# Numbering sorted tokens by partition first and chunk second, with running sums on GpSimd, in a convolution, attention and mixture-of-experts kernel

## The chip, the cores and the metric

The kernel runs on one core of one Trainium2 chip. The metric is device time in microseconds of one execution. The engines are named as the profile names them: PE (TensorE; its weight loads are PEld), DVE (VectorE), ACT (ScalarE), POOL (GpSimd) and SP (SyncE, which only issues transfers here).

## The reference, cut to what matters

The input is 32 images of 128 channels and 56 x 56 pixels, so 3136 tokens an image.

```
x = x + conv3x3(sign(groupnorm(x)), sign(w)) * Alpha
t = tokens of x                                    # 3136 an image, 128 wide
t = t + q(ln(t)) * sum over tokens of k(ln(t)) * v(ln(t))
...
p = softmax(ln(t) @ router_w + router_b)           # 8 experts
top_p, top_i = top_k(p, 2); top_p /= sum(top_p)
t = t + sum over the two of top_p * (ln(t) @ expert_w[top_i] + expert_b[top_i])
```

Each token goes through the two experts of its own choice, so it belongs to one of 8 * 7 / 2 = 28 unordered pairs of experts. In what order tokens of one pair are worked on is free.

## The kernel before, in words

**Tiling.** The tokens of an image stand in 25 chunks of up to 128 tokens, one token a partition (`n_ck` = 25). The layers up to the router run image by image: convolution in 7 strips (L642), transposes to tokens, statistics, the gram matrix (L744), the projection (L863), the router on DVE (L949 on).

**Two ways through the experts.** The first 8 or 12 chunks of an image, and all chunks of images 28 to 31, are done densely: all eight experts for each token, with gates that are 0 for six of them (`gated`, L1141, and `ff`, L1159). The other 17 chunks (images 0 to 15) or 13 chunks (images 16 to 27) are sorted by pair over a group of images (groups of 8, 8, 8 and 4): each token's row of 132 floats is written by an indirect transfer, which GpSimd issues, to its place in a buffer of rows in HBM (`scatter`, L1365, one for each chunk, 428 in all). Once a group is complete, tiles of 128 rows of one pair are read back, go through two experts alone (L1687), are stored, and are then fetched back into token order by another 428 indirect transfers (`gather`, L1444), turned (`back_turn`, L1459) and stored.

**The place of a token.** The steps that the change touches compute it, once for each of the 28 images with sorted chunks; `n_sort` is 17 or 13:

- `pair_of` (L1236, DVE): the number of the token's pair, and last `hot` (L1256): for each chunk 28 columns, 1 in the column of the token's pair, in bf16.
- `hot_blocks` (L1263): sums of four chunks of `hot`, on POOL in images 0 to 7 (three adds, L1268 and L1270), on DVE from image 8 on (one reduction, L1272).
- `places` (L1274, PE): for each chunk and pair the place of the next token in one PSUM tile of 504 or 392 columns. A product with the triangle `before` (L1278) counts the tokens on lower partitions of the same chunk; two products add the counts of the images before, as a high and a low bf16 part (L1281); products with `ones_h` (L1293) add earlier chunks, by single chunks within a block of four and by `hot_sum` for whole blocks: 17 of them for 17 chunks, 13 for 13. So places are numbered chunk by chunk, and within a chunk by partition.
- `count_on` (ACT, L1303 and L1304) and `count_rest` (DVE, L1307): the last 28 columns are the counts to carry on.
- `row_numbers` (DVE, L1309): `hot` times `places`, read from PSUM, summed over the 28 columns (L1315), gives the row (L1318).
- `row_add` (ACT) and `scatter` (POOL) follow.

`list_1` (L1550, DVE) reads the counts when the last image of a group is counted and lists the tiles.

**What sets the order.** Every engine runs its queue in order. The order of all queues comes from a planner, `in_order` (L116), which lays out 12116 steps by due times, costs and waits: each `at(due, key, engine, cost, do, after=, take=, free=)` declares a step, `take` and `free` the buffers of a ring such as the five PSUM banks `ps`. The costs are estimates written in the code: `hot_blocks` has 2.0 us on POOL and 0.048 * n_sort on DVE, `places` 0.3 + 0.08 * n_sort, a gather or a scatter 1.5 us. A step whose cost differs on the chip keeps its place in the queue; its engine or those after it then wait. Gathers land in a ring of `back` buffers (room for 12 in the plan), and at most four indirect transfers are under way at a time.

Of the kernel before, what the change touches and what calls it, by code (L numbers as in the profile page):

```python
# [54 lines left out]
C = 128  # L55
# [20 lines left out]
    mybir.EngineType.Pool,  # L76
    mybir.EngineType.SP,
}
ON_POOL = 8
NEWTON = 3  # L80
IN_FLIGHT = 4
HELD, LOADS, LOAD_LANDS = 3, 4, 10.0
# [103 lines left out]
def conv_attn_moe_kernel(  # L186
# [357 lines left out]
    def plan_image(i: int):  # L544
# [688 lines left out]
        hot = hot_all[:, most - n_sort :, :]  # L1233
        n_full = n_sort // PER

        def pair_of():  # L1236
            high, low, pair = (
# [16 lines left out]
            yield  # L1254
            shape = [C, n_sort, N_PAIR]
            nc.vector.tensor_tensor(  # L1256
                hot[:, :n_sort, :],
                mark.unsqueeze(2).to_broadcast(shape),
                pair_no.unsqueeze(1).to_broadcast(shape),
                ALU.is_equal,  # L1260
            )

        def hot_blocks():  # L1263
            t = hot[:, : n_full * PER, :].rearrange("p (b k) q -> p b k q", k=PER)
            total = hot_sum[:, :n_full, :]
            with nc.allow_low_precision(reason="numbers up to four"):
                if i < ON_POOL:
                    nc.gpsimd.tensor_tensor(total, t[:, :, 0], t[:, :, 1], ALU.add)  # L1268
                    for k in range(2, PER):
                        nc.gpsimd.tensor_tensor(total, total, t[:, :, k], ALU.add)  # L1270
                else:
                    nc.vector.tensor_reduce(total, t.rearrange("p b k q -> p b q k"), AX.X, ALU.add)  # L1272

        def places():  # L1274


            p = ps.tile([C, n_sort + 1, N_PAIR], F32, tag="ps", name=f"places_{i}")
            nc.tensor.matmul(p, lhsT=before, rhs=hot, start=True, stop=False)  # L1278
            if not first_of_group:
                for j in range(2):  # L1280
                    nc.tensor.matmul(  # L1281
                        p,
                        lhsT=ones_h[:1],
                        rhs=count_h[:1, j].unsqueeze(1).to_broadcast([1, n_sort + 1, N_PAIR]),
                        start=False,
                        stop=False,
                    )

            counted = [(hot[:, c, :], c + 1, min(n_sort + 1, c // PER * PER + PER)) for c in range(n_sort)]
            counted += [(hot_sum[:, b, :], (b + 1) * PER, n_sort + 1) for b in range(n_full)]  # L1290
            counted = [(t, lo, hi) for t, lo, hi in counted if lo < hi]
            for t, lo, hi in counted:
                nc.tensor.matmul(  # L1293
                    p[:, lo:hi, :],
                    lhsT=ones_h,
                    rhs=t.unsqueeze(1).to_broadcast([C, hi - lo, N_PAIR]),
                    start=False,
                    stop=lo == counted[-1][1] and hi == counted[-1][2],
                )
            d["places"] = p  # L1300

        def count_on():
            nc.scalar.copy(count, d["places"][:, n_sort, :])  # L1303
            nc.scalar.copy(count_h[:, 0], d["places"][:, n_sort, :])  # L1304

        def count_rest():
            nc.vector.tensor_sub(count_h[:, 1], count, count_h[:, 0])  # L1307

        def row_numbers():  # L1309
            shape = [C, n_sort, N_PAIR]  # L1310
            own = spool.tile(shape, F32, tag="own", bufs=1, name=f"own_{i}")
# [50 lines left out]
        def scatter(c):  # L1362
# [15 lines left out]
            after=[("route_3", i), ("row_numbers", i - 1), ("places", i - 1), ("result_rows", i - 13)],  # L1378
        )
        at(  # L1380
            s + 132.5, ("hot_blocks", i), "POOL" if i < ON_POOL else "DVE",
            2.0 if i < ON_POOL else 0.048 * n_sort, hot_blocks, after=[("pair_of", i)],
        )
        at(
            s + 133, ("places", i), "PE", 0.3 + 0.08 * n_sort, places,
            after=[("hot_blocks", i), ("count_rest", i - 1), ("list_1", group - 1)], take=["ps"],
        )
        at(s + 135, ("count_rest", i), "DVE", 0.10, count_rest, after=[("count_on", i)])
        at(s + 134, ("count_on", i), "ACT", 0.22, count_on, after=[("places", i)])
# [488 lines left out]
```

## Time and profile before

| | |
|---|---|
| median of 3 runs | 2259.04 us (2249.86 to 2283.94) |
| profiled execution | 2270.18 us |
| its span | 2268.4 us |
| granted TensorE clock, mean | 0.975 |
| POOL scatters (L1365) | 428, 524.3 us, mean 1225 ns |
| POOL gathers (L1444) | 428, 485.4 us, mean 1134 ns |
| DVE gating products (L1141) | 384, 450.7 us, mean 1180 ns |
| `hot` (L1256), `own` (L1313), `place` (L1315), medians | 590, 642, 650 ns |
| `count`, `count_h` (L1303, L1304), medians | 182, 188 ns |

The span is the time from the first to the last instruction in the trace. Busy time is the sum over an engine's own work; waits, branches and the issue of transfers on SP don't count[...]. "Idle before, released by" names what an engine waited for. Matmuls are pipelined, so several overlap within their stated lengths.

### The profile page before, as it was taken

The page shows a single profiled execution, that of the slowest core. Times are in us where ns is not written, and L with a number is a line of the kernel's source. Part 1 is how long each engine was busy: PE and PEld are TensorE (multiplying, and loading weights), DVE is VectorE, ACT ScalarE, POOL GpSimd, SP SyncE. Part 2 cuts the span into 40 slices and gives each one's busy share as a digit, 9 for nine tenths or more (in the row PEclk, how much of TensorE's full clock was granted, in tenths as well). Part 3 has the DMA queues.
Part 4 walks back from the last instruction along what each step waited for, and adds up shares of the span by engine and source line. Part 5 has one row for each costly group of instructions (what it writes and reads, how often), then busy time and mean ns, then how long its engine had stood idle before and what let it go on. Part 6 is the DMA issues. An engine that isn't in the chain of part 4 may idle for free.

```text
span 2268.4 us, 45320 instructions
## 1 busy us (share of the span) xinstructions
PE 2103.4 (93%) x12074; PEld 1449.1 (64%) x12074; DVE 1970.1 (87%) x6074; ACT 1531.2 (68%) x4917; POOL 1041.1 (46%) x1013
## 2 busy tenths in 40 slices
PE   5899999899999999789999999988999999999888
PEld 2666656557777776457676776655676666676544
DVE  4899999999989999688888889988898798789865
ACT  5667776668888887468777867655877776574311
POOL 3044443333433325466443644676654446233563
PEclk9989999999999999899999999999999999999999
DMA  4155544465665565377667766667767777878788
GB/s 166 30 175 177 167 153 141 138 184 184 203 186 165 176 181 168 110 219 252 194 202 220 226 198 202 215 214 240 225 195 232 217 203 247 249 214 270 222 278 273
DMA packets 324364, 448.58 MB, mean 198 GB/s; under 512 B 61832, under 2 KB 222128, under 8 KB 324112
## 3 DMA queue, kind: packets, MB, share of 16 engines
q1 hardware_dynamic: 294384, 382.80, 54.7%
q0 software_dynamic: 28144, 56.14, 8.2%
q10 hardware_dynamic: 1584, 6.75, 0.8%
q8 instruction: 102, 1.67, 0.3%
q14 instruction: 150, 1.23, 0.2%
HBM read 319.51 MB, written 126.00 MB: 196 GB/s over the span
## 4 chain that ended last, share of the span: by engine, by line
PE 42%; DVE 5%; DMA 3%; issue 2%; ACT 2%; another core or an unknown queue 1%; SPq 0%; POOL 0%; DVEq 0%; ACTq 0%; POOLq 0%
PE ff L1159 14%; PE to L1687 7%; PE cv L642 6%; PE q L863 3%; PE gram L744 3%; PE turn L1669 2%; PE back_ps L1459 2%; PE xt L667 2%; DVE gated L1141 1%; DMA back<-res,res_no 1%; PE l L1114 1%; DMA out_dram<-o 1%; PE ff L1153 1%; DMA bc<-gp 0%
## 5 line engine op out<-in xcount | busy, mean ns | idle before, releaser
L1365 POOL DMA_INDIRECT rows<-tok,row_no x428 | 524.3, 1225 | 570.5 <-ACT tok L1358 235.8
L1159 PE MATMUL ff<-gated,ew_d 128*128 128x512 f32 (+1 forms) x1536 | 711.5, 592 | 23.8 <-DVE gated L1141 19.8
L1444 POOL DMA_INDIRECT back<-res,res_no x428 | 485.4, 1134 | 464.1 <-PE back_ps L1459 264.1
L1141 DVE TENSOR_TENSOR gated<-tt,bc 128x1024 f32<-128x1024 f32 x384 | 450.7, 1180 | 92.2 <-PE ff L1159 29.9
L642 PE MATMUL cv<-xs,w_bin 128*128 128x440 bf16 (+3 forms) x2016 | 429.8, 362 | 18.5 <-ACT xs L599 10.0
L1159 PEld LDWEIGHTS ff<-gated,ew_d 128*128 128x128 f32 x1536 | 274.5, 193 | 258.6 <-issue 202.2
L1705 ACT ACTIVATE v<-to,t_in 128x128 f32<-128x128 f32 x528 | 255.3, 484 | 138.1 <-PE to L1687 74.6
L642 PEld LDWEIGHTS <-w_bin 128*128 128x128 bf16 x2016 | 200.1, 100 | 187.8 <-issue 38.3
L1687 PEld LDWEIGHTS to<-ew_s,turned 128*128 128x128 f32 x2112 | 260.8, 194 | 57.8 <-issue 32.4
L877 ACT ACTIVATE qs<-q,r 128x136 f32<-128x136 f32 (+1 forms) x800 | 247.6, 406 | 70.3 <-PE q L863 35.1
L1687 PE MATMUL to<-ew_s,turned 128*128 x2112 | 273.3, 279 | 18.2 <-ACT turned L1675 8.1
L735 ACT ACTIVATE y<-tok,r 128x128 f32<-128x128 f32 (+1 forms) x800 | 257.0, 428 | 24.3 <-PE gram L744 10.4
L863 PE MATMUL q<-move,x 128*128 128x144 f32 (+1 forms) x1600 | 239.9, 295 | 12.7 <-issue 3.7
L863 PEld LDWEIGHTS q<-move,x 128*128 128x128 f32 (+1 forms) x1600 | 213.6, 193 | 42.4 <-issue 21.1
L744 PEld LDWEIGHTS gram<-y 128*128 128x128 f32 (+1 forms) x1600 | 203.3, 192 | 53.9 <-issue 40.4
L744 PE MATMUL gram<-y 128*128 128x129 f32 (+1 forms) x1600 | 217.8, 281 | 12.9 <-issue 8.1
L682 DVE BATCH_NORM_STATS2 st<-tok 128x6 f32<-128x128 f32 (+1 forms) x800 | 185.4, 279 | 31.9 <-ACT tok L673 26.9
L1712 ACT ACTIVATE w<-to,t_in 128x128 f32<-128x128 f32 x528 | 208.6, 395 | 0.0
L893 DVE BATCH_NORM_STATS2 st<-tok 128x6 f32<-128x128 f32 (+1 forms) x800 | 198.1, 284 | 6.3
L673 ACT COPY tok<-xt 128x512 f32<-128x512 f32 (+1 forms) x224 | 121.2, 561 | 99.9 <-PE xt L667 71.6
L653 DVE SCALAR_TENSOR_TENSOR x<-cv,alpha_col,x 128x448 f32<-128x448 f32 x224 | 151.3, 676 | 40.1 <-PE cv L642 7.2
L890 DVE TENSOR_TENSOR tok<-tok,qs 128x408 f32<-128x408 f32 (+1 forms) x288 | 156.1, 542 | 29.4 <-ACT tok L882 24.1
(229 smaller groups left out, 2896.0 us busy)
## 6 DMA issues: line engine op xcount, KB each, us to landing
bc<-gp SPq DMA_DIRECT2D x368, 512.0 KB
x<-in_x_dram SPq DMA_DIRECT2D x116, 392.0 KB
t_in<-rows SPq DMA_DIRECT2D x528, 66.0 KB
res<-v SPq DMA_DIRECT2D x132, 256.0 KB
out_dram<-o SPq DMA_DIRECT2D x100, 256.0 KB
out_dram<-tt SPq DMA_DIRECT2D x92, 256.0 KB
rows<-zeros SPq DMA_DIRECT2D x116, 66.0 KB
rows<-tok,row_no POOLq DMA_INDIRECT x428
```

The costliest lines, as they stand in the source:

```text
L642: nc.tensor.matmul(cv[:, r0:r1, c0:c1], lhsT=w_bin[:, t, :], rhs=xs[:, b * ROWS + dy + r0 : b * ROWS + dy + r1, dx + c0 : dx + c1], start= ...
L735: nc.scalar.mul(y[:n, j, :C], d["tok"][:n, c, :C], d["r1"][:n, c : c + 1])
L744: nc.tensor.matmul(d["gram"], lhsT=y[:n, j, :C], rhs=y[:n, j, :], start=(c == 0), stop=(c == n_ck - 1),)
L863: nc.tensor.matmul(p[:n, k, :], lhsT=d["x"][:, c * C : c * C + n], rhs=move, start=True, stop=True,)
L877: nc.scalar.mul(qs[:n, k, :], p[:n, k, : C + N_EXP], d["r1"][:n, c : c + 1])
L1141: nc.vector.tensor_tensor(g[:, :, :n], d["tt", b][:, :n].unsqueeze(1).to_broadcast([C, 2, n]), d.pop(("bc", b, k))[:, :, :n], ALU.mult,)
L1159: nc.tensor.matmul(d["ff", b][:, :n], lhsT=ew_d[:, e * C : (e + 1) * C], rhs=g[:, j, :n], start=False, stop=(e == N_EXP - 1),)
L1365: dma = nc.gpsimd.indirect_dma_start(out=groups[group]["rows"], out_offset=bass.IndirectOffsetOnAxis(ap=d["row_no"][:n, c - n_dense : c - ...
L1444: dma = nc.gpsimd.indirect_dma_start(out=d["back", c][:n, :], out_offset=None, in_=groups[group]["res"][: quads_of(group) * WIDE, :], in_o ...
L1687: nc.tensor.matmul(p[:, k, j, :], lhsT=t[:, n * C : (n + 1) * C], rhs=ew_s[:, bass.ds(d["cols", q][j][n], C)], start=True, stop=True,)
L1705: nc.scalar.activation(d["v", q][:, n, :], p[:, k, 0, :], AF.Identity, bias=row[:, C + 2 : C + 3], scale=row[:, C : C + 1],)
L1712: nc.scalar.mul(d["w", q][:, n, :], p[:, k, 1, :], row[:, C + 1 : C + 2])
```

## The change

Places are numbered by partition first and by chunk second. POOL adds up `hot` chunk by chunk in `run`, 28 columns at a time (`run_on`, 17 or 13 adds, each of which reads what the one before it wrote), so that `run[:, c]` holds, for each partition, the tokens of each pair in earlier chunks, and the last one the total of the partition. `places` then needs only that last total: one product with `before` for the tokens on lower partitions, one with `ones_h` for the counts, and, but for the first image of a group, one product of 33 rows that adds the earlier images' counts, the high part from row 0 and the low part from row 32 of `count_h`. The PSUM tile has 56 columns. ACT copies both halves to `counts`, which frees the bank. POOL then adds the partition's start to all of `run` (`ranks`, one addition of 476 or 364 fp32 columns), and `row_numbers` multiplies `hot` with this from SBUF. `hot_blocks` and `hot_sum` are gone, on POOL as on DVE. The planner has costs of 0.20 (`RUN`) and 0.10 us (`RANK`) a chunk for the two new POOL steps, 0.25 for `places`, 0.35 for `count_on`.

In the changed program PE has 80 products for the places instead of 504. The planner lays out all queues again, so the order of other steps moves too. On POOL the adds and `ranks` stand ahead of an image's scatters; from image 14 on they stand between gathers of the group before. In the program each add but the first waits on a semaphore of POOL itself.

```diff
-ON_POOL = 8
+RUN, RANK = 0.20, 0.10
...
-    count = const.tile([C, N_PAIR], F32, name="count")
-    count_h = const.tile([C, 2, N_PAIR], BF16, name="count_h")
+    counts = const.tile([C, 2, N_PAIR], F32, name="counts")
+    count = counts[:, 1]
+    n_part = C // 4 + 1
+    count_h = const.tile([n_part, N_PAIR], BF16, name="count_h")
+    both = const.tile([n_part, C], BF16, name="both")
...
-    hot_all = const.tile([C, most + 1, N_PAIR], BF16, name="hot")
-    hot_sum = const.tile([C, most // PER, N_PAIR], BF16, name="hot_sum")
+    hot_all = const.tile([C, most, N_PAIR], BF16, name="hot")
+    run_all = const.tile([C, most + 1, N_PAIR], BF16, name="run")
 
     def prepare_sorted():
-        nc.gpsimd.memset(hot_all, 0.0)
-        nc.vector.memset(count_h, 0.0)
+        nc.gpsimd.memset(run_all[:, 0], 0.0)
+        nc.vector.memset(both, 0.0)
+        nc.vector.memset(both[:1], 1.0)
+        nc.vector.memset(both[n_part - 1 :], 1.0)
...
-        def hot_blocks():
-            t = hot[:, : n_full * PER, :].rearrange("p (b k) q -> p b k q", k=PER)
-            total = hot_sum[:, :n_full, :]
-            with nc.allow_low_precision(reason="numbers up to four"):
-                if i < ON_POOL:
-                    nc.gpsimd.tensor_tensor(total, t[:, :, 0], t[:, :, 1], ALU.add)
-                    for k in range(2, PER):
-                        nc.gpsimd.tensor_tensor(total, total, t[:, :, k], ALU.add)
-                else:
-                    nc.vector.tensor_reduce(total, t.rearrange("p b k q -> p b q k"), AX.X, ALU.add)
+        def run_on():
+
+            with nc.allow_low_precision(reason="numbers up to the chunks of an image"):
+                for c in range(n_sort):
+                    nc.gpsimd.tensor_tensor(run[:, c + 1], run[:, c], hot[:, c], ALU.add)
 
         def places():
-            p = ps.tile([C, n_sort + 1, N_PAIR], F32, tag="ps", name=f"places_{i}")
-            nc.tensor.matmul(p, lhsT=before, rhs=hot, start=True, stop=False)
+            p = ps.tile([C, 2, N_PAIR], F32, tag="ps", name=f"places_{i}")
             if not first_of_group:
-                for j in range(2):
...
+                nc.tensor.matmul(
+                    p,
+                    lhsT=both,
+                    rhs=count_h.unsqueeze(1).to_broadcast([n_part, 2, N_PAIR]),
+                    start=True,
+                    stop=False,
+                )
+            for j, lhs in enumerate((before, ones_h)):
+                nc.tensor.matmul(
+                    p[:, j], lhsT=lhs, rhs=run[:, n_sort], start=first_of_group, stop=first_of_group or j == 1
                 )
             d["places"] = p
 
         def count_on():
-            nc.scalar.copy(count, d["places"][:, n_sort, :])
-            nc.scalar.copy(count_h[:, 0], d["places"][:, n_sort, :])
+            nc.scalar.copy(counts, d["places"])
+            nc.scalar.copy(count_h, d.pop("places")[:n_part, 1])
 
         def count_rest():
-            nc.vector.tensor_sub(count_h[:, 1], count, count_h[:, 0])
+            last = slice(n_part - 1, n_part)
+            nc.vector.tensor_sub(count_h[last], count[last], count_h[last])
+
+        def ranks():
+            shape = [C, n_sort, N_PAIR]
+            d["own"] = spool.tile(shape, F32, tag="own", bufs=1, name=f"own_{i}")
+            nc.gpsimd.tensor_tensor(
+                d["own"], run[:, :n_sort], counts[:, 0].unsqueeze(1).to_broadcast(shape), ALU.add
+            )
 
         def row_numbers():
...
-            nc.vector.tensor_tensor(own, hot[:, :n_sort, :], d.pop("places")[:, :n_sort, :], ALU.mult)
+            nc.vector.tensor_tensor(own, hot, own, ALU.mult)
...
+            s + 132.5, ("run_on", i), "POOL", RUN * n_sort, run_on,
+            after=[("pair_of", i), ("places", i - 1), ("ranks", i - 1)],
...
+            s + 133, ("places", i), "PE", 0.25, places,
+            after=[("run_on", i), ("count_rest", i - 1), ("list_1", group - 1)], take=["ps"],
...
+            s + 134, ("count_on", i), "ACT", 0.35, count_on,
+            after=[("places", i), ("ranks", i - 1), ("list_1", group - 1)],
+            free=[("ps", ("places", i))],
...
+        at(s + 135, ("count_rest", i), "DVE", 0.08, count_rest, after=[("count_on", i)])
+        at(
+            s + 135, ("ranks", i), "POOL", RANK * n_sort, ranks,
+            after=[("count_on", i), ("row_numbers", i - 1)],
+        )
...
             s + 137, ("row_numbers", i), "DVE", [0.033 * n_sort, 0.034 * n_sort, 0.09], row_numbers,
-            after=[("places", i), ("count_on", i), ("scatter", i - 2, n_ck - 1)],
-            free=[("ps", ("places", i))],
+            after=[("ranks", i), ("scatter", i - 2, n_ck - 1)],
```

More of the change, by code (lines that the diff above doesn't have):

```diff
@@ L1232, in plan_image @@
         sort = slice(n_dense, n_ck)
-        hot = hot_all[:, most - n_sort :, :]
-        n_full = n_sort // PER
+        hot, run = hot_all[:, :n_sort], run_all[:, : n_sort + 1]
         def pair_of():
@@ L1256, in pair_of @@
             nc.vector.tensor_tensor(
-                hot[:, :n_sort, :],
+                hot,
                 mark.unsqueeze(2).to_broadcast(shape),
@@ L1274, in places @@
         def places():
-            p = ps.tile([C, n_sort + 1, N_PAIR], F32, tag="ps", name=f"places_{i}")
-            nc.tensor.matmul(p, lhsT=before, rhs=hot, start=True, stop=False)
+            p = ps.tile([C, 2, N_PAIR], F32, tag="ps", name=f"places_{i}")
             if not first_of_group:
-                for j in range(2):
[L1281 to L1298, printed above, removed]
+                nc.tensor.matmul(
+                    p,
[4 more added lines that the diff above has]
+                )
@@ L1302, in count_on @@
         def count_on():
-            nc.scalar.copy(count, d["places"][:, n_sort, :])
-            nc.scalar.copy(count_h[:, 0], d["places"][:, n_sort, :])
+            nc.scalar.copy(counts, d["places"])
+            nc.scalar.copy(count_h, d.pop("places")[:n_part, 1])
         def count_rest():
-            nc.vector.tensor_sub(count_h[:, 1], count, count_h[:, 0])
+            last = slice(n_part - 1, n_part)
[6 more added lines that the diff above has]
+            )
         def row_numbers():
-            shape = [C, n_sort, N_PAIR]
-            own = spool.tile(shape, F32, tag="own", bufs=1, name=f"own_{i}")
+            own = d.pop("own")
             place = spool.tile([C, n_sort], F32, tag="place", bufs=13, name=f"place_{i}")
-            nc.vector.tensor_tensor(own, hot[:, :n_sort, :], d.pop("places")[:, :n_sort, :], ALU.mult)
+            nc.vector.tensor_tensor(own, hot, own, ALU.mult)
             yield
@@ L1380, in plan_image @@
         at(
-            s + 132.5, ("hot_blocks", i), "POOL" if i < ON_POOL else "DVE",
-            2.0 if i < ON_POOL else 0.048 * n_sort, hot_blocks, after=[("pair_of", i)],
-        )
-        at(
-            s + 133, ("places", i), "PE", 0.3 + 0.08 * n_sort, places,
-            after=[("hot_blocks", i), ("count_rest", i - 1), ("list_1", group - 1)], take=["ps"],
-        )
-        at(s + 135, ("count_rest", i), "DVE", 0.10, count_rest, after=[("count_on", i)])
-        at(s + 134, ("count_on", i), "ACT", 0.22, count_on, after=[("places", i)])
+            s + 132.5, ("run_on", i), "POOL", RUN * n_sort, run_on,
+            after=[("pair_of", i), ("places", i - 1), ("ranks", i - 1)],
+        )
+        at(
+            s + 133, ("places", i), "PE", 0.25, places,
+            after=[("run_on", i), ("count_rest", i - 1), ("list_1", group - 1)], take=["ps"],
+        )
+        at(
[4 more added lines that the diff above has]
+        at(s + 135, ("count_rest", i), "DVE", 0.08, count_rest, after=[("count_on", i)])
+        at(
+            s + 135, ("ranks", i), "POOL", RANK * n_sort, ranks,
+            after=[("count_on", i), ("row_numbers", i - 1)],
+        )
         at(
             s + 137, ("row_numbers", i), "DVE", [0.033 * n_sort, 0.034 * n_sort, 0.09], row_numbers,
-            after=[("places", i), ("count_on", i), ("scatter", i - 2, n_ck - 1)],
-            free=[("ps", ("places", i))],
+            after=[("ranks", i), ("scatter", i - 2, n_ck - 1)],
         )
```

## The prediction

> **What bounds the kernel now.** I read the page's busy shares and 40 slices first, then busy time in five stretches, then the rows of the tiles that the change touches, and last the order of time around one image.
>
> ```profile
> PE 2103.4 (93%) x12074; PEld 1449.1 (64%) x12074; DVE 1970.1 (87%) x6074; ACT 1531.2 (68%) x4917; POOL 1041.1 (46%) x1013
> ...
> PE   5899999899999999789999999988999999999888
> ...
> POOL 3044443333433325466443644676654446233563
> ```
>
> PE is busy from the third slice to the end and its granted clock stands at 0.8 or more in every slice, so PE sets the pace: 165 us of the 2268.4 us span are idle, most of that at the start and in the last stretch. DVE is close behind (298 us idle), POOL has half its time free. The chain that ended last, followed back over the later half of the span, agrees: PE has 42% of the span in it, DVE 5%, POOL 0%; the lines it names are expert, conv, projection and gram products. What the change takes off PE is therefore worth nearly its own length, unless PE then waits for something new.
>
> The products for the places on PE alone, their busy time summed over five stretches that cover the span:
>
> ```profile
> sum 2269.00, PE 43.77; mean PE 8.75
> ```
>
> and by line (count: shortest/median/longest in ns, first and last start in us, forms):
>
> ```profile
> L1278 PE MATMUL places<-hot,before x28: 328/375/627, 110.5 to 1831.4; 128*128 128x504 bf16 x16, 128*128 128x392 bf16 x12
> L1281 PE MATMUL places<-count_h,ones_h x48: 325/372/382, 156.6 to 1831.9; 1*128 1x504 bf16 x28, 1*128 1x392 bf16 x20
> L1293 PE MATMUL places<-hot,ones_h x328: 174/189/279, 110.9 to 1832.4; 128*128 128x28 bf16 x64, 128*128 128x84 bf16 x56, 128*128 128x56 bf16 x44
> L1293 PE MATMUL places<-hot_sum,ones_h x100: 187/237/488, 111.6 to 1832.6; 128*128 128x280 bf16 x28, 128*128 128x168 bf16 x28, 128*128 128x56 bf16 x28, 128*128 128x392 bf16 x16
> ```
>
> So 504 products hold PE for 43.8 us, 1.9% of the span. PE's idle time before the first of them is 0.4 us in all 28 images together: their operands are there when PE comes to them.
>
> **What the added adds cost.** Today GpSimd sums one-hots for eight images only, three adds of 112 columns each:
>
> ```profile
> L1272 DVE TENSOR_REDUCE hot_sum<-hot x20: 707/730/928, 515.1 to 1829.2; 128x84 bf16<-128x336 bf16 x12, 128x112 bf16<-128x448 bf16 x8
> L1270 POOL TENSOR_TENSOR hot_sum<-hot_sum,hot x16: 384/432/1420, 107.5 to 452.7; 128x112 bf16<-128x112 bf16 x16
> L1268 POOL TENSOR_TENSOR hot_sum<-hot x8: 373/376/602, 107.0 to 451.7; 128x112 bf16<-128x112 bf16 x8
> ```
>
> And what happens around them, in order of time (start and length in us), for the first image and then for the second:
>
> ```profile
> 107.04 0.38 POOL L1268 TENSOR_TENSOR hot_sum<-hot 128x112 bf16<-128x112 bf16 x1 [78.57 <-DVE gate L981]
> 107.49 0.98 POOL L1270 TENSOR_TENSOR hot_sum<-hot_sum,hot 128x112 bf16<-128x112 bf16 x2
> ...
> 153.67 1.21 DVE L1141 TENSOR_TENSOR gated<-tt,bc 128x1024 f32<-128x1024 f32 x1
> 153.70 1.42 POOL L1270 TENSOR_TENSOR hot_sum<-hot_sum,hot 128x112 bf16<-128x112 bf16 x1
> 154.80 0.37 DVE L1346 TENSOR_TENSOR tok<-a,m_one 128x34 f32<-128x34 f32 x1
> ```
>
> Two things to see. Each add waits for the one before it: starts are 0.45 us apart where the add itself takes 0.38, a gap of 0.07. And GpSimd and DVE stop each other: an add that met the gating product (two SBUF inputs) took 1.42 instead of 0.38, and the next DVE instruction, half beneath the add, took 0.37 instead of its usual 0.18. Nearly every one of the 24 adds lengthens one DVE instruction by about 0.19 us.
>
> **What the Trainium skill says.** "GPSIMD Engine Reference", section 3.1, gives 4497 ns for a GpSimd add of 2048 fp32 elements, 2.2 ns an element; with it a 112-column add has 0.24 us of elements and 0.13 of fixed cost, which fits 0.376. Its section 8 (Key points) says that GpSimd shares its SBUF interfaces with VectorE and contends with instructions that have two SBUF inputs: the pair at 153.67 shows it. "Perfetto Trace Analysis", section "GPSIMD Engine Instruction", advises timing GpSimd by start-to-start spacing rather than by reported spans; so I price the adds by spacing.
>
> **The change part by part.**
>
> PE. Removed: 504 products, 43.8 us. Added: 80 (three an image, two in the four first of a group) of 28 or 56 columns. One such alone takes 0.19 us, and in a row they follow at 0.55/13 = 0.04 us (13 products in 0.55 us at 157.11); I take 0.19 + 2 x 0.10 = 0.39 an image, 11 us. Net **-33 us**, on the path. Bounds -28 (no overlap of the three) to -38 (full overlap).
>
> DVE. Removed: 20 reductions of 0.730, -14.6 us. The product of marks and places keeps its columns (0.64, now from SBUF), the subtraction its 0.18. Two small memsets at the start: nothing. Added: being stopped. 428 running adds that hold the port between 0.05 us (by columns, 28 of 112) and 0.19 us (all of it fixed), and 28 rank additions of 476 or 364 columns, 0.13 + 476 x 2.2 ns = 1.2 us (0.9); the planner's 0.10 a chunk, 1.7 us, is the upper bound. If DVE wants the port 7 times in 10: 428 x 0.10 x 0.7 + 28 x 1.1 x 0.7 = 30 + 22 = 52, from 15 to 90. Net about **+37 us on DVE**; it has 298 us idle, and its gating products feed PE, so I let a quarter through: +9, between 0 and +30.
>
> ACT. Two copies an image as before, 56 columns instead of 28 in one (0.18 now): nothing, hidden by 32% idle. The ps bank comes free at these copies, no longer at DVE's first part of row_numbers, 1 to 3 us sooner; the view of this tile lists 3.6 us in which PE waited for its readers, so this is worth -2, at most -4.
>
> POOL. The eight hot_sum sets go (11 us). 428 adds of 28 columns: by columns 0.376 - 84 x 2.2 ns = 0.19, plus the gap 0.07 = 0.27 us apart; no dearer than the 112-column ones, 0.45. DVE's traffic lengthened the 24 adds by 0.09 on average over 0.376; I take 0.32. That is 5.4 us for 17 chunks and 4.2 for 13, where the planner laid the queues out with RUN = 0.20: 3.4 and 2.6. Sum 137 us, ranks 31: POOL to some 1200 us, 53%. Queued behind run_on, which waits for DVE's marks, are scatters of the same image, and from image 14 on gathers of the group before; these have a ring of 12 back buffers ahead of PE, and POOL's longest wait is for PE (264 us, for the turning of those rows), so POOL runs ahead and the gathers keep their cover.
>
> The new wait. PE's products now need all of run_on, which starts when DVE's marks (L1256) end. Today the first product starts 1.7 to 7.7 us after the marks, 3.4 on average. The changed order puts it later by what run_on is planned to take beyond hot_blocks: 1.4 us in images 0 to 7 (3.4 for 2.0), 2.6 in 8 to 15 (3.4 for 0.8), 2.0 in 16 to 27 (2.6 for 0.6). PE is then there after 4.8, 6.0 and 5.4 us. At 0.32 us an add and 0.3 for two semaphore hops, run_on needs 5.7 us for 17 chunks and 4.5 for 13. So PE waits 0.9 us in each of the first 8 images (7), nothing on average in the next 8, but with a scatter of 1 to 2 us around it half a us (4), and in the last 12 some 0.3 by the same scatter and 0.3 for a gather that POOL is just issuing (7). About 18 us of waiting in the whole, queued behind which are conv, expert and gram products; ACT's copies and DVE's row_numbers wait the same time. Three quarters reach the end: **+13**, bounds 0 (0.27 us an add) to +86 (0.45, below).
>
> DMA. Rows go to other places in the same buffers, same count and size of packets (528 bytes a row): 0, with 10 us either way, since no run here shows other row orders. SP's steps are the same.
>
> Sum: -33 + 9 + 13 - 2 = **-13 us**. The profiled execution took 2270.18 us with its 2268.4 us span, 11 us above the median of the three runs shown, 2259.04 (2249.86 to 2283.94). -13 gives 2257 for it, and 2246 against the median.
>
> **The rivals.**
>
> 1. PE gets all of it. The adds run at 0.27, PE never waits, DVE's contention falls into its idle time and the 14.6 us of reductions and the banks shorten other engines' waits too: -38 - 10 - 4 = -52, 2207 us. For it: PE at 93%, 54% of POOL idle. Against it: the visible mutual stops.
>
> 2. The other side: GpSimd becomes the link that PE waits for. If an add takes 0.50 us (the spacing seen, 0.45, being fixed price rather than columns, and a little of DVE's interference), run_on needs 8.8 us and 6.8. PE waits 4.0 us in 8 images, 2.8 in 8 and 1.4 plus half a gather (0.65) in 12: 32 + 22 + 25 = 79. With DVE at +12, less 33: +58, 2317 us. It decides from an add of about 0.37 us on (break-even: waits of 35 us, three quarters of them through), and passes 2% at about 0.46. For it: 0.45 is the one spacing seen. Against it: that is for four times the columns.
>
> 3. The change does little because the planner's new order gives elsewhere what it takes: all queues are laid out anew from the first image. That gives between -20 and +20 beside the sum, and lies inside the first case.
>
> **How the numbers follow.** 2% is about what a measurement of this kernel can tell from no change: 45 us. The likeliest case (2246, own range 2215 to 2275, with the third rival in it) has 0.46, rival 1 0.34, rival 2 0.20. Faster by over 2% means below 2214: 0.34; slower, above 2304: 0.20. The range of 8 in 10 takes in most of rival 1 and what lies between the first case and rival 2, whose far part is left out: 2196 to 2304.
>
> **What would show it.** Right: products for the places near 10 us of PE in all; running adds starting 0.27 to 0.36 us apart; PE idle before the first product 10 to 30 us in total, put down to POOL; DVE's small instructions longer by some 0.1 us beside the adds, its busy time up by 20 to 50 us. Wrong: adds 0.4 us apart or more and PE idle there over 60 us (rival 2); no PE wait there and a PE busy time down by 33 with the span down as much or more (rival 1); or a difference that comes from stretches after image 27, where none of the changed steps run.

## Result, and the profile after

| | before | after |
|---|---|---|
| median, us | 2258.35 (4 runs, 2249.86 to 2283.94) | 2289.22 (4 runs, 2288.41 to 2296.36) |
| profiled execution / its span, us | 2270.18 / 2268.4 | 2296.36 / 2294.7 |
| granted TensorE clock, mean | 0.975 | 0.966 |
| PE busy without the places, us | 2059.6 | 2069.7 |
| PE busy with the places, us | 43.8 | 10.0 |
| PE idle (span less busy), us | 165.0 | 215.0 |

The ratio of after to before is 1.0156 (95% interval 1.0126 to 1.0186): the change makes the kernel slower by about 35 us. The forecast was 13 us faster. Ratios are of the means of those executions that are within 1.5% of the fastest of their kernel, so the 2283.94 of before is not in them (the medians of the table differ by 31 us), and the profiles of experiments 2 and 9 show an execution slower than that. The last three rows of the table add up to the span in each column, so they say where the 26 us between the two profiled executions come from: 34 less of places, 10 more of all other products, 50 more of idle time.

The page of the changed kernel, busy time by engine, then PE's 40 slices, then the shares of the chain that ended last:

```profile
PE 2079.7 (91%) x11650; PEld 1441.2 (63%) x11650; DVE 1982.4 (86%) x6056; ACT 1532.8 (67%) x4917; POOL 1194.4 (52%) x1445
...
PE   5889889988999999798999999899889988999888
...
PE 47%; DVE 30%; issue 6%; DMA 5%; ACT 5%; POOL 5%; another core or an unknown queue 2%; SPq 0%; DVEq 0%; ACTq 0%; POOLq 0%
```

PE's row, which was 9 almost throughout, has 8 in more slices of the stretch with sorting. The chain before was followed over the later half of its span alone, so its shares can't be compared with these; here POOL has 5%, nearly all of it the running adds.

The view of the tile `places`: rows of its products, then the time its engine sat idle before it, by releaser (us, times):

```profile
L1286 PE MATMUL places<-run,before x28: 174/174/188, 116.9 to 1852.0; 128*128 128x28 bf16 x28
...
L1278 PE MATMUL places<-count_h,both x24: 188/196/197, 162.0 to 1849.1; 33*128 33x56 bf16 x24
...
  POOL run L1271: 48.5, 21
```

In 21 of the 28 images PE stands at these products until the last running add is done, 48.5 us in all. Before, what stood ahead of the first product of all 28 images was, in the view of its line (L1278):

```profile
  DVE h L1343: 0.2, 1
  DVE gate L979: 0.2, 1
```

So this one wait is about as large as the whole growth of PE's idle time. The adds themselves, in the view of the tile `run` (shortest/median/longest in ns):

```profile
L1271 POOL TENSOR_TENSOR run<-run,hot x428: 231/237/2131, 109.3 to 1851.7; 128x28 bf16<-128x28 bf16 x143
L1302 POOL TENSOR_TENSOR own<-run,counts x28: 882/1088/1522, 117.4 to 1854.7; 128x476 f32<-128x476 bf16 x16, 128x364 f32<-128x364 bf16 x12
```

An add takes 237 ns at the median (the shortest 231), but the page's mean is 311 ns, and the mean distance from start to start is 0.392 us: 0.32 to 0.33 in the quietest images, up to 0.61 in the busiest. What this does in the second image, in order of time (start, length in us; in brackets the idle time before, and its releaser):

```profile
157.22 0.65 DVE L1260 TENSOR_TENSOR hot<-mark,pair_no 128x476 bf16<-128x476 f32 x1
158.01 6.39 POOL L1271 TENSOR_TENSOR run<-run,hot 128x28 bf16<-128x28 bf16 x17 [4.54 <-DVE hot L1260]
159.88 1.21 DVE L1146 TENSOR_TENSOR gated<-tt,bc 128x1024 f32<-128x1024 f32 x1
161.96 0.20 PE L1278 MATMUL places<-count_h,both 33*128 33x56 bf16 x1
164.45 0.18 PE L1286 MATMUL places<-run,before 128*128 128x28 bf16 x1 [2.30 <-POOL run L1271]
164.75 0.20 ACT L1292 COPY counts<-places 128x56 f32<-128x56 f32 x1 [3.73 <-PE places L1286]
165.04 1.09 POOL L1302 TENSOR_TENSOR own<-run,counts 128x476 f32<-128x476 bf16 x1 [0.64 <-ACT count_h L1293]
165.64 0.53 DVE L1297 TENSOR_TENSOR count_h<-counts,count_h 1x28 bf16<-1x28 f32 x1
```

POOL starts as soon as the marks are there and works without a break, but 17 adds last 6.4 us (0.376 each). PE does the counts' product at 161.96, and then its queue stands for 2.3 us. ACT, which has the copy of the result next in its queue, stands for 3.7. DVE's subtraction at the end, which lies beneath the rank addition, takes 0.53 instead of 0.18.

POOL doesn't always start so soon. The 25th image (image 24):

```profile
1595.71 0.47 DVE L1260 TENSOR_TENSOR hot<-mark,pair_no 128x364 bf16<-128x364 f32 x1
1608.33 3.23 POOL L1447 DMA_INDIRECT back<-res,res_no  x1 [0.30 <-issue]
1611.59 4.03 POOL L1271 TENSOR_TENSOR run<-run,hot 128x28 bf16<-128x28 bf16 x13
1615.66 0.18 PE L1286 MATMUL places<-run,before 128*128 128x28 bf16 x1 [5.91 <-POOL run L1271]
```

The marks are there at 1596.2, but POOL is still issuing gathers of the group before and comes to the adds 15.4 us later. The adds themselves are as quick here as in any image (0.32 us apart), and PE stands for 5.9 us all the same.

### The profile page after: what moved, and what is told of

The parts are those of the page before. It is cut to its first block, busy times and chain, and to the rows that moved or that the text cites. A ratio compares the mean times of both kernels' runs of the same rounds, so it can differ in the third digit from the quotient of the medians.

```text
span 2294.7 us, 44948 instructions
## 1 busy us (share of the span) xinstructions
PE 2079.7 (91%) x11650; PEld 1441.2 (63%) x11650; DVE 1982.4 (86%) x6056; ACT 1532.8 (67%) x4917; POOL 1194.4 (52%) x1445
## 4 chain that ended last, share of the span: by engine, by line
PE 47%; DVE 30%; issue 6%; DMA 5%; ACT 5%; POOL 5%; another core or an unknown queue 2%; SPq 0%; DVEq 0%; ACTq 0%; POOLq 0%
PE ff L1164 15%; PE cv L647 8%; PE to L1690 7%; DVE gated L1146 6%; PE q L868 5%; POOL run L1271 4%; PE gram L749 3%; DVE st L898 3%; DVE st L687 3%; DVE tok L895 2%; DVE x L658 2%; PE xt L672 2%; PE turn L1672 2%; DVE tok L820 2%
## 5 line engine op out<-in xcount | busy, mean ns | idle before, releaser
L1361 POOL DMA_INDIRECT rows<-tok,row_no x428 | 519.0, 1213 | 373.8 <-ACT tok L1354 174.9
L1447 POOL DMA_INDIRECT back<-res,res_no x428 | 493.5, 1153 | 360.0 <-PE back_ps L1462 181.3
L1146 DVE TENSOR_TENSOR gated<-tt,bc 128x1024 f32<-128x1024 f32 x384 | 450.6, 1179 | 75.1 <-PE ff L1164 30.9
L1271 POOL TENSOR_TENSOR run<-run,hot 128x28 bf16<-128x28 bf16 x428 | 133.2, 311 | 322.7 <-DVE hot L1260 137.9
L868 PE MATMUL q<-move,x 128*128 128x144 f32 (+1 forms) x1600 | 245.9, 301 | 8.5 <-issue 2.7
L868 PEld LDWEIGHTS q<-move,x 128*128 128x128 f32 (+1 forms) x1600 | 221.3, 199 | 39.3 <-issue 20.1
L749 PEld LDWEIGHTS gram<-y 128*128 128x128 f32 (+1 forms) x1600 | 198.1, 191 | 40.4 <-issue 31.0
L749 PE MATMUL gram<-y 128*128 128x129 f32 (+1 forms) x1600 | 210.6, 277 | 3.4 <-issue 3.4
```

Source lines behind the costliest of these rows:

```text
L749: nc.tensor.matmul(d["gram"], lhsT=y[:n, j, :C], rhs=y[:n, j, :], start=(c == 0), stop=(c == n_ck - 1),)
L868: nc.tensor.matmul(p[:n, k, :], lhsT=d["x"][:, c * C : c * C + n], rhs=move, start=True, stop=True,)
L1146: nc.vector.tensor_tensor(g[:, :, :n], d["tt", b][:, :n].unsqueeze(1).to_broadcast([C, 2, n]), d.pop(("bc", b, k))[:, :, :n], ALU.mult,)
L1361: dma = nc.gpsimd.indirect_dma_start(out=groups[group]["rows"], out_offset=bass.IndirectOffsetOnAxis(ap=d["row_no"][:n, c - n_dense : c - ...
L1447: dma = nc.gpsimd.indirect_dma_start(out=d["back", c][:n, :], out_offset=None, in_=groups[group]["res"][: quads_of(group) * WIDE, :], in_o ...
```

## The experiments

Theory A: PE's wait for the running adds, in queues laid out for 0.20 us an add, is what the change costs. Theory B: it is the SBUF port that GpSimd's new work takes from DVE. Theory C: it is the new order of the queues. All ratios are to the kernel before, run on the same chip, with 95% intervals.

**1. The planner's price of an add doubled.** The same instructions as after; run_on alone is planned longer, so the planner puts the places later into PE's queue.

```diff
-RUN, RANK = 0.20, 0.10
+RUN, RANK = 0.40, 0.10
```

> The changed kernel with one constant changed: the planner's price of a running add is 0.40 us instead of 0.20, so that the products for the places are laid into PE's queue later. Theory A (PE waits because the adds take 0.39 us and the queues were laid out for 0.20): PE's wait for the running sums falls from 48 us to under 15 us, the adds still start 0.39 us apart, and the time falls by 25 to 45 us, to 2245 to 2265. Theory B (GpSimd's adds hold up DVE through the shared port, and PE's wait is a symptom): the wait moves or shrinks but the time stays above 2275. Theory C (the new order alone): any time between 2240 and 2300, with no tie to the wait.

Measured: 0.999 (0.9968 to 1.0013), 2265.17 us beside 2266.04. Two lines of the view of `places`, one on what PE waited for, one on who waited for the places:

```profile
  POOL run L1271: 5.2, 2
...
  POOL own L1302: 43.5, 20
```

The adds are as slow as in after (0.40 us apart), but PE's wait falls from 48.5 to 5.2 us, and the loss is gone. The wait has changed sides: POOL now stands 43.5 us at its rank addition until PE and ACT bring the counts; in after the same line read 8.1. The time is at the upper end of what A expected, and below B's 2275. This supports A, with the reservation that the order changes too.

**2. A further shift, 0.55.** The same edit with `RUN = 0.55`.

> As the run with 0.40, but with 0.55 us an add. Theory A: PE's wait under 5 us; no further gain in time, within 10 us of the run with 0.40, or a little slower because scatters are laid out later. Theory B: like the changed kernel, above 2275. Theory C: no order among 0.20, 0.40 and 0.55.

Measured: 1.0073 (1.0049 to 1.0098). PE's wait fell to 2.0 us and the time rose all the same, by 0.8% or 19 us over experiment 1, where A expected 10 us at most or a little more. So waiting for the sums isn't everything: something else in this layout of the queues costs time. What it is was not tried; POOL stood 101.8 us at its rank additions in it, beside 43.5 in experiment 1.

**3. The total by DVE.** PE gets the totals from a reduction on DVE, and POOL's adds, one fewer an image, serve the ranks alone. An add is planned at 0.40 us, as in experiment 1.

```diff
+        def hot_total():
...
+                nc.vector.tensor_reduce(total, hot.rearrange("p c q -> p q c"), AX.X, ALU.add)
...
-                    p[:, j], lhsT=lhs, rhs=run[:, n_sort], start=first_of_group, stop=first_of_group or j == 1
+                    p[:, j], lhsT=lhs, rhs=total, start=first_of_group, stop=first_of_group or j == 1
```

> The changed kernel with the total of each partition taken by one DVE reduction (0.7 us), so that PE's products wait for DVE alone and GpSimd's running sums, one add fewer, are needed only for the rank addition; the planner's price of an add is 0.40. Theory A: PE waits under 5 us before these products, the time is at or below that of the run with 0.40, 2235 to 2260, as DVE has 20 us more work. Theory B: above 2275, since the adds are all still there.

Measured: 1.011 (1.0038 to 1.0181), a miss for A, which expected no loss. PE waited only 4.0 us for the totals. In exchange DVE has 28 reductions of 0.87 us median, 24.3 us together, and its busy time rose to 1995.0 (1973.9 in experiment 1). PE was idle for 210.9 us, against 180.9 in experiment 1, and its longest wait in total was for DVE's gating products (L1147), 39.1 us beside 28.3. So part of the loss goes with a later DVE; how much is the layout's, this run doesn't tell.

**4. The adds alone.** The kernel before, with 428 running adds and 28 wide additions on POOL whose results nobody reads, planned at 0.40 and 0.10 us a chunk.

```diff
+        def run_on():
...
+                for c in range(n_sort):
+                    nc.gpsimd.tensor_tensor(run_all[:, c + 1], run_all[:, c], hot[:, c], ALU.add)
```

> The kernel before with the running adds and one addition of 17 or 13 times 28 columns an image on GpSimd beside it, whose result nobody reads; PE's 504 products stay, and nothing but GpSimd's own queue and the shared port can cost time. Theory A: within 12 us of the kernel before. Theory B: slower than before by 25 us or more, with DVE's busy time up by that order.

**5. The same plan with empty steps.** As experiment 4, but both POOL steps issue nothing: what is left is the order that the planner makes around them.

```diff
         def run_on():
...
-                for c in range(n_sort):
-                    nc.gpsimd.tensor_tensor(run_all[:, c + 1], run_all[:, c], hot[:, c], ALU.add)
+            pass
```

> The control of the run with idle adds: the same steps with the same prices in the planner, so the same order on every queue, but with no GpSimd instruction in them. If the idle adds cost 27 us by holding up DVE and GpSimd (theory B), this is within 8 us of the kernel before. If the new order alone costs it (theory C), this is 20 to 30 us above before, like the run with idle adds.

Measured: 1.0121 (1.0065 to 1.0177) for experiment 4 and 1.0084 (1.0051 to 1.0117) for 5. Busy time over the whole span, first in experiment 4, then in 5:

```profile
sum 2290.00, PE 2108.74 PEld 1449.28 DVE 1991.01 ACT 1533.74 POOL 1212.20; mean PE 2108.74 PEld 1449.28 DVE 1991.01 ACT 1533.74 POOL 1212.20
```

```profile
sum 2278.00, PE 2099.51 PEld 1446.38 DVE 1969.96 ACT 1533.49 POOL 1054.54; mean PE 2099.51 PEld 1446.38 DVE 1969.96 ACT 1533.49 POOL 1054.54
```

Taken alone, experiment 4 is what B expected (25 us or more, DVE's busy time up by that order); experiment 5 takes most of it back. In the same order, 456 additions lengthen DVE's work by 21.0 us and the run by 0.37% or 8 us (the intervals overlap, so it may be nothing). The order alone costs 0.84%, 19 us, without one addition. So B shows in DVE's busy time and is small or nothing in the run's; C is the larger of the two here.

**6. How far the order alone reaches.** The kernel before with another planned price for one ACT step, so that the same instructions stand in another order.

```diff
-        at(s + 134, ("count_on", i), "ACT", 0.22, count_on, after=[("places", i)])
+        at(s + 134, ("count_on", i), "ACT", 0.35, count_on, after=[("places", i)])
```

> The kernel before with one planner price that does not matter moved, 0.35 instead of 0.22 us for the two copies of the counts on ACT: no instruction is added or left out, only the order differs. It measures what another order is worth. Theories A and B: within 10 us of before. Theory C: 15 us or more away from before, either way.

Measured: 0.9977 (0.9956 to 0.9998). This is 5 us, where C expected 15 or more. With experiment 5, layouts that differ in nothing else lie between -0.2% and +0.8%.

**7. More adds in the same order.** After, with the first add of each image issued seven times: 168 additions more (the repeats write the same values again). No queue but POOL's changes.

```diff
-                for c in range(n_sort):
+                for c in [0] * 6 + list(range(n_sort)):
                     nc.gpsimd.tensor_tensor(run[:, c + 1], run[:, c], hot[:, c], ALU.add)
```

> The changed kernel, same order on PE, DVE, ACT and SP, with the first running add of each image issued seven times instead of once: 168 more adds, about 2.3 us more an image ahead of PE's products. Theory A: PE waits 50 to 65 us more in 25 or so images and the time rises by 40 to 65, to 2330 to 2355. Theory B: 168 more adds on top of 428 cost a third of what those cost, some 10 us. Theory C: no change.

Measured: 1.0455 (1.0412 to 1.0498), 3.0% or 68 us above after, 0.40 us for each of the 168 adds. The wait in the view of `places`:

```profile
  POOL run L1271: 90.9, 27
```

It grew by 42.4 us, from 48.5. The run grew by more, 68 us, and by more than A expected (2355 us at most, 2361.84 measured). Of the 63 us between the two profiled executions 36 are idle time of PE and 26 its products other than the places (2095.8 beside 2069.7), at a mean clock of 0.954 instead of 0.966. DVE's busy time didn't grow (1982.2 beside 1982.4).

**8. Fewer links in the chain, in the same order.** After, with the sums in two levels: three wide adds over all blocks of four chunks (the fourth chunk's goes straight into the block's end), then block by block, so that the total needs 7 dependent adds (17 chunks) instead of 17; two wide adds fill in the ranks once the total is there. PE, DVE, ACT and SP have after's exact queues.

```diff
-                for c in range(n_sort):
-                    nc.gpsimd.tensor_tensor(run[:, c + 1], run[:, c], hot[:, c], ALU.add)
...
+                add(s[:, :, 2], t[:, :, 0], t[:, :, 1], ALU.add)
+                add(s[:, :, 3], s[:, :, 2], t[:, :, 2], ALU.add)
+                add(run[:, PER : n_in + 1 : PER], s[:, :, 3], t[:, :, 3], ALU.add)
+                for c in range(2 * PER, n_in + 1, PER):
+                    add(run[:, c], run[:, c], run[:, c - PER], ALU.add)
+                add(run[:, n_in + 1], run[:, n_in], hot[:, n_in], ALU.add)
...
```

> The changed kernel in its own order on PE, DVE, ACT and SP, with the running sums done in two levels: three adds over all blocks of four chunks at once, three or two adds from block to block and one for the last chunk, 2.6 us in a row instead of 6.5, and two more wide adds after PE has its total. Theory A: PE's wait for the sums falls from 48 us to under 10, and the time by 35 to 50, to 2240 to 2255, about 1% below before. Theory B: GpSimd's adds are fewer but not much shorter in all (5.0 us an image for 7.7), so a third of 27 us comes back: above 2270. Theory C: no change, as the order is the same.

Here `t` is `hot` and `s` is `run`, seen as blocks of `PER` = 4 chunks.

Measured: 0.9987 (0.9961 to 1.0013), 1.7% or 38 us below after (some 9 us either way by the two intervals). POOL's second image, in order of time:

```profile
153.29 0.40 POOL L1272 TENSOR_TENSOR run<-hot 128x112 bf16<-128x112 bf16 x1 [3.27 <-DVE hot L1260]
153.77 0.40 POOL L1273 TENSOR_TENSOR run<-run,hot 128x112 bf16<-128x112 bf16 x1
154.25 0.40 POOL L1274 TENSOR_TENSOR run<-run,hot 128x112 bf16<-128x112 bf16 x1
154.72 2.00 POOL L1276 TENSOR_TENSOR run<-run 128x28 bf16<-128x28 bf16 x3
156.80 0.24 POOL L1277 TENSOR_TENSOR run<-run,hot 128x28 bf16<-128x28 bf16 x1
```

and what PE waited for at the places, over all images:

```profile
  POOL run L1277: 3.7, 2
```

The total is there 3.75 us after the first add's start instead of 6.39, although the block adds met one of DVE's gating products (L1146, 1.21 us from 155.09 on) and took 2.00 us for the three. PE's wait is 44.8 us shorter and the run 38 us, in the same order on the four other engines. The busy times show what is left of B as a rival here:

```profile
PE 2072.9 (92%) x11650; PEld 1432.4 (64%) x11650; DVE 1983.2 (88%) x6056; ACT 1532.3 (68%) x4917; POOL 1144.5 (51%) x1257
```

POOL works 50 us less than in after, but DVE is no less busy (1982.4 there), so it isn't the port that gave the 38 us back. This settles A as the largest part: the wait is what separates after from a change of no effect.

**9. The products twice.** The kernel before, with all 504 products for the places issued twice (the second set starts the accumulation anew), DVE, ACT and SP in the same order: what PE's busy time of this kind is worth.

```diff
-            nc.tensor.matmul(p, lhsT=before, rhs=hot, start=True, stop=False)
+            for _ in range(2):
+                nc.tensor.matmul(p, lhsT=before, rhs=hot, start=True, stop=False)
...
```

> The kernel before with its 504 products for the places issued twice in a row (the second set overwrites the first), in the same order on DVE, ACT and SP: 44 us more for PE and nothing else. It measures what taking PE's products away is worth in a fixed order. If PE's time counts fully, the time rises by 40 to 50 us (1.8 to 2.2%). If half of it lies in gaps where PE would wait anyway, by 15 to 30.

Measured: 1.0098 (1.0062 to 1.0134), 22 us (14 to 31), and these products' busy time (us of the span, busy time and count of PE, clock, DMA share, GB/s):

```profile
0.00:2329.00 2329.00, 83.15 (x1008) 0.97 0.62 193
```

That is 39.4 us more than the 43.8 of before, for 22 us of run: 0.56 of their length (0.36 to 0.77). Where the rest goes isn't shown; time in which PE would have waited for others is the likely place.

**10. Can the saving be kept?** The two-level sums in other layouts: with price 0.25 and 0.07 a chunk; with the ranks' two adds as a step of their own behind the total (prices 0.19 and 0.075 a chunk beside it); and in experiment 1's exact order.

```diff
-RUN, RANK = 0.20, 0.10
+RUN, RANK = 0.25, 0.07
```

> The two-level sums with the planner's price of a chunk at 0.25 instead of 0.20 us and of the rank addition at 0.07 instead of 0.10. Theory A: PE's wait under 5 us, time within 10 us of the two-level kernel. Theory C: up to 20 us either way at the same wait.

```diff
         at(
+            s + 133.5, ("run_rest", i), "POOL", 0.085 * n_sort, run_rest, after=[("run_on", i)],
+        )
...
```

> The two-level sums with the part that PE waits for (2.6 us) and the part that only the ranks need (1.1 us) as two steps of the planner with prices near the measured ones. Theory A: PE's wait for the sums stays under 10 us, and the time is that of the two-level kernel or up to 20 us less, 2235 to 2260. Theory C: another order, so up to 20 us either way at the same wait.

```diff
-RUN, RANK = 0.20, 0.10
+RUN, RANK = 0.40, 0.10
```

> The two-level sums in the exact order on PE, DVE, ACT and SP of the run whose planner price was 0.40 (where PE waited 5 us for the sums). Only GpSimd's own work differs, about 5 us an image instead of 7.7. Theory A alone: within 6 us of that run, 2260 to 2268, as there is no wait left to take away. If the shared port and GpSimd's queue cost more than that, 10 us or more below it.

Measured: 1.0053 (1.0026 to 1.008), 1.0049 (1.0027 to 1.0072) and 1.004 (1.0011 to 1.007), with PE's waits for the sums at 3.8, 11.1 and 3.2 us. None is better than experiment 8, and all three are 11 to 15 us above what A expected of them. So the wait can be short and the kernel still half a per cent slower: that experiment 8 is level with before is in part the fortune of its layout. In experiment 1's order the shorter chain brought nothing where PE hardly waits any more; why it came out half a per cent higher there (1.004 beside 0.999, on another chip, the intervals just touching) stays open. No version that I tried is clearly faster than the kernel before: the lowest are experiment 6 (0.9977), which has nothing of the change in it, and experiment 8 (0.9987).

## Why the prediction was wrong

**The step that failed is "The new wait".** It had 18 us of waiting, three quarters of them through: +13. Measured were 48.5 us, and experiment 8 shows what they cost: 38 us for 44.8 of wait, in the same order. Two terms in it were mis-sized.

First the adds: "I take 0.32" for the spacing; the mean was 0.392. I had split the 0.376 us of a 112-column add with a rate worked out from a price for 2048 fp32 elements, which gave 0.19 us for 28 columns; the 0.13 of fixed cost was the remainder of that split, so that it "fits 0.376" tested nothing. The trace after has 0.237, so 84 columns fewer save 0.14 and not 0.19, and the rest is a fixed price. DVE's interference, 0.09 on the 24 adds of before, of which I took 0.05, was 0.074 (311 less 237 ns).

Second, what stands ahead of the adds in POOL's queue. With 0.392 the step's own sum gives 17 us for images 0 to 7, 8 for images 8 to 15 and, with its 0.3 for a scatter and 0.3 for a gather that POOL is just issuing, 7 for the last twelve: 32 us. PE's wait in these three groups, by the view of L1286:

```profile
  POOL run L1271: 11.0, 7
...
  POOL run L1271: 15.1, 6
...
  POOL run L1271: 22.4, 8
```

The last twelve waited three times what they were given, and 16.2 of their 22.4 us fall in four images (16, 17, 22 and 24) in which POOL came to the adds 2.5 to 15.4 us after the marks, busy with gathers, as shown above for image 24. A whole row of gathers can stand there, not the rest of one. In images 8 to 15 PE came 4.9 us after the marks and not 6.0; in images 0 to 7 it came after 4.8, as forecast, and the adds were 0.35 us apart.

Rival 2 put the point from which GpSimd decides at "about 0.37 us", so the measured spacing lies on its side. It was the right mechanism, and with 0.50 its size was too large (79 us of wait, 2317 us). Spacing and wait fell between the signs given for the likeliest case (up to 0.36 us, 10 to 30 us) and those for rival 2 (0.4 us, over 60 us).

**PE, -33 on the path.** The busy time was right: 43.77 to 9.98, -33.8. "What the change takes off PE is therefore worth nearly its own length" was wrong. By experiment 9, 0.56 of it counts, about -19 us (-12 to -26). This is a rate for adding such products; that it holds for taking them away is assumed. The reading behind it was off too: of PE's 165 us of idle time before, 98 lie between 200 and 1860 us, so most of it is not at the start and in the last stretch.

**DVE, +37 busy, +9 on the path.** Busy went from 1970.1 to 1982.4 although the 20 reductions, 15.9 us together, are gone, so +28 of being stopped instead of 52. The stops sit where it was said, in small instructions beneath POOL's: the subtraction `count_h`, 0.18 or 0.19 us before, is now up to 1.65 us long.

```profile
L1297 DVE TENSOR_TENSOR count_h<-counts,count_h x28: 176/177/1650, 117.5 to 1853.4; 1x28 bf16<-1x28 f32 x28
```

Experiments 4 and 5 put the price of all this at 8 us of run, near the 9 taken. That is luck in part: the stops were half as long and a larger share of them went through, and by the intervals the 8 may be nothing. The rank addition (1088 ns for "1.2 us") and POOL's load (1194.4 us, for "some 1200") were right too, as was that the gathers keep their cover: PE waited 4.1 us for gathered rows, 4.0 before. The bank's -2 fits as well: PE's waits for the readers of `places` went from 3.6 to 0.8 us, and ACT's busy time, taken as unchanged, grew by 1.6 us.

**The order.** Rival 3 gave the new layout -20 to +20 us and I put it inside the first case at zero. Experiment 5 found +19 for one such layout, experiment 6 -5 for another. In after's own layout no run has it apart from the port: experiment 8, in that order, stands at -3 us with the wait gone, and less the -19 for PE's products leaves +16 for order and port together.

The sum by these terms: -19 for the products, +38 for the wait with what it does to the clock, +16 for order and port: +35, which is 1.0156. It closes by construction, since the +16 is what is left over (+9 to +23 by the range of the -19) and not measured by itself. Rows landing in another order were taken at 0 and weren't tried alone; they are within that +16.

## What to carry to other kernels

Before moving work from PE to a slower engine, count the dependent instructions between its input and the first one that PE needs: a chain of 17 small adds costs 17 times the spacing in a trace, fixed price and interference in it, and three wide adds with a short chain behind gave the same total in 0.6 of the time. Count also what can stand ahead of that chain in the slower engine's queue. Price a moved step in the planner by measured spacing, since a step that takes twice its planned time turns into a wait of an in-order queue (0.20 planned and 0.39 taken was worth 1.7% here); once the wait is gone, prices nearer to the measured ones brought nothing more, as experiment 10 shows. And where an order is laid out anew by every edit, run the new order with empty steps before reading anything into less than 1%.

## What the runs showed of the hardware

A wait of PE can cost more than its length. In the 23rd image (image 22) of the changed kernel PE's queue stands from 1472.9 us for 5.9 us, until the running adds are done; in stretches of a few microseconds (bounds in us, length, PE's busy time and count, granted clock, DMA share, GB/s):

```profile
1466.00:1470.00 4.00, 4.00 (x24) 1.00 0.35 88
1470.00:1472.90 2.90, 2.90 (x20) 1.00 0.48 146
1472.90:1478.80 5.90, 0.02 (x2) 0.68 0.37 125
1478.80:1485.20 6.40, 6.40 (x26) 0.50 0.20 62
1485.20:1490.00 4.80, 4.80 (x31) 1.00 0.66 198
```

The clock falls during the wait, stays at 0.50 for the next 6.4 us, though PE is busy throughout, and is then back at 1.00. If it knows only 1.00 and 0.50 in the stretch with 0.68, it fell about 2.1 us after PE stopped (an estimate: 3.8 of the 5.9 us at half give 0.68). The Trainium skill describes this in "TensorE: Matmul & The Clock Gate", section "What's actually happening": the clock is let through by half after an idle window of about 3.4 us and released again by activity. The trace agrees with the half, but not with 3.4 us without work: here some 2.1 us were enough.

Over whole runs the mean clock falls, broadly, as PE's idle time grows. From experiment 6 over before and after to experiment 7 the idle time is 144.8, 165.0, 215.0 and 251.2 us, the mean clock 0.980, 0.975, 0.966 and 0.954, and the products other than the places take 2046.7, 2059.6, 2069.7 and 2095.8 us. Experiment 3, with 4.0 us of waiting for the totals but 210.9 us of idle time, has 0.963 and 2087.4 us. So the 10 us of longer products in after can't be put down to the 48.5 us of waits alone. Nor does a wait always cost more than its length: 42.4 us more of it cost 68 us in experiment 7, and 44.8 us less gave back 38 in experiment 8.

Another surprise is the size of the stops: an addition of 28 columns, 237 ns at the median, took 2131 ns once in the changed kernel, at 1545.1 us, beside four DVE instructions of which one is a gating product of 1.21 us.
